# A two-layer convolution and window-attention kernel: layer 0's TensorE work regrouped by tile shape, with the normalisation moved ahead

## The chip, the core and the metric

The kernel runs on one core of a Trainium2 chip. The metric is the device time of one execution in microseconds; before the change its median over three runs is 3106.57 us (3105.86 to 3109.45). Engines are named as in the profile: PE is TensorE (PEld its weight loads), DVE is VectorE, ACT is ScalarE, POOL is GpSimd, SP is SyncE, which issues most DMAs. L403 is line 403 of the kernel before.

## The reference, cut to what matters

The input x is (2, 128, 256, 256) in float32: two images of 128 channels. Layer 0 adds halo attention to x, layer 1 adds the product of two small convolutions. Only layer 0 is touched by the change.

```python
WS, OWS, HEADS, DH = 8, 12, 4, 32       # 8x8 windows of queries, 12x12 of keys
def layer0(x, W_qkv, W_out, rel_height, rel_width):
    qkv = einsum('bchw,oc->bohw', x, W_qkv)
    q, k, v = split(qkv, 3, axis=1)
    q = windows(q) * DH ** -0.5; k = unfold_windows(k); v = unfold_windows(v)
    attn = q @ k.T + rel_pos_emb(q, rel_height, rel_width) + FIXED_MASK
    out = softmax(attn) @ v
    return einsum('bchw,oc->bohw', out, W_out)
x = x + layer0(group_norm(x), ...)
x = x + layer1(group_norm(x), ...)      # 5x1 convolution, depthwise 3x1, times a dilated 1x3
```

FIXED_MASK leaves each query only the keys whose row and column offsets have one parity. So the pixels fall into classes by the parities of row and column, and a query meets the 6x6 keys of its class.

## The kernel before, in words

**Strips and units.** Layer 0 (attention_fast) goes over 64 strips of 8 image rows, 32 for each image. A strip k has two units u = 2k and 2k + 1, one for each row parity r; 128 units in all. A unit holds both column parities c and 16 pairs of windows. Everything is float32, and each matmul of the code is two matmul and two weight-load instructions on TensorE.

**What a unit does.** The order on every engine is the order in the code (manual_schedule, L538), so the loop at L545 is the order of the work:

- In even units, load_rows fetches strip k + 2 (SP, 1280 KB), and normalise(k + 1) writes the normalised strip k + 1 by cells into one of two buffers xn: a GpSimd copy of the old rows (L308), four VectorE operations of 512 columns (L317), two copies of shared columns (L322, L323).
- In odd units of the first image, input_stats takes statistics of a strip of the second image (VectorE, four operations, L117), and load_next issues the next such load into the one buffer sx. Three strips' statistics stand elsewhere (units 4 and 8).
- by_place (GpSimd, four copies, L331) lays half of strip k + 1 out as xq for its coefficients; old_keys (GpSimd, L342) copies keys that two strips share.
- biases (L443): 16 matmuls in 32x64 tiles add the relative-position coefficients and the masks into the score banks.
- scores (L459): 64 matmuls in 64x64 tiles; ScalarE takes the exponentials in four pieces (L468).
- values (L424): 16 matmuls of 128 columns with the whole 128x128 array; ScalarE and VectorE copy one half of each bank to the tile vt (L430).
- coefficients (L403) of strip k + 1: 16 matmuls of 64 columns in 128x64 tiles into one bank; ScalarE (L412) and then VectorE (L416) copy one half each.
- attend (L484): 64 matmuls of 66 columns in 128x32 tiles, in three banks; VectorE divides by the sums (L490, L491), and turn transposes (L502).
- queries and keys of unit u + 1 and project of unit u (all L349): products with the whole array. in_parts cuts each bank's 512 columns into several matmuls: queries into three (one in the first unit of an image), keys and projection into two. result_stats takes the statistics of the unit before, and project adds the input (VectorE, L518) and stores the unit by SP.

All banks of values, coefficients, attention, queries, keys and projection come from one pool of four PSUM banks (tag pj), given out in turn: each needs the release of the bank given out four before it. At unit 8 VectorE computes six small sums of layer 1's weights (Weights.sums, L609 to L612). The two group norms that fall into this loop (of x of the second image, and of the first image's result) run in seven steps, one at each call of step().

**What follows.** convolutions_fast is layer 1; it starts when layer 0's last strips are stored.

## Time and profile before

| what | value |
|---|---|
| median of 3 runs | 3106.57 us |
| the profiled execution's own span | 3104.3 us (clock 0.996) |
| median of the runs above this span | 2.3 us |
| TensorE busy, matmuls and as many weight loads | 96%, 52,006 each |
| VectorE, ScalarE, GpSimd busy | 82%, 55%, 18% |
| first unit's biases; layer 1's first matmul | 107.9 us; 2103.4 us |
| a usual unit of layer 0 | 15.47 us |
| packets that bring TensorE's instructions (queue q8) | 412, 6.75 MB |

How to read it: the profile gives one execution. A view called the chain of work follows back from the last instruction what released each step, and shows the pieces with their start and length; "issue" in it is time in which the engine waited for nothing that the profile shows. The groups view gives busy time and mean length for each line of code, the waits view who waited for whom, and the timeline the instructions in order of time. Matmuls are pipelined, and their ends are modelled, so I compare starts with starts.

### The profile page before, as it was taken

What the parts mean: (1) busy time and instruction counts of PE and PEld (TensorE: products, weight loads), DVE (VectorE), ACT (ScalarE), POOL (GpSimd) and SP (SyncE); (2) the same over time, 40 slices, a digit from 0 to 9 for tenths busy, and PEclk for the clock granted to TensorE, in tenths of its full rate; (3) what the DMA queues carried; (4) which work ended last, traced back from release to release, by engine and by line L of the source; (5) the groups of instructions that cost most, each with busy time, mean ns of one, the idle gap of its engine ahead of it and who ended that gap; (6) DMA issues with size and microseconds to landing.
All of it is one profiled execution on the core that took longest, in us unless ns stands there. A gap on an engine that the chain in (4) does not pass through costs nothing.

```text
span 3104.3 us, 116029 instructions
## 1 busy us (share of the span) xinstructions
PE 2971.1 (96%) x52006; PEld 2248.5 (72%) x52006; DVE 2533.3 (82%) x4092; ACT 1711.4 (55%) x2673; POOL 569.0 (18%) x921
## 2 busy tenths in 40 slices
PE   0799999999999999999999999998999999999998
PEld 0688888888888888888888888884444444444443
DVE  8788888888888878777777777767999999999998
ACT  0455555555555555555555555555666665666664
POOL 2222222222222222222222222210000000000001
PEclk9999999999999999999999999999999999999999
DMA  9433333333333222222222222215788888888886
GB/s 395 160 125 128 111 115 111 115 112 115 111 115 112 84 71 87 72 86 72 88 71 87 71 88 71 84 37 168 206 217 213 221 216 213 222 215 214 217 217 167
DMA packets 137401, 434.75 MB, mean 140 GB/s; under 512 B 12993, under 2 KB 87617, under 8 KB 104385
## 3 DMA queue, kind: packets, MB, share of 16 engines
q1 hardware_dynamic: 127824, 361.18, 34.1%
q0 software_dynamic: 9072, 66.06, 11.5%
q8 instruction: 412, 6.75, 0.9%
q14 instruction: 93, 0.75, 0.1%
HBM read 284.59 MB, written 134.22 MB: 135 GB/s over the span
## 4 chain that ended last, share of the span: by engine, by line
PE 92%; DVE 2%; issue 1%; DMA 1%; ACT 0%; POOL 0%; SPq 0%; DVEq 0%; POOLq 0%; ACTq 0%
PE f_pv L424 15%; PE a_e L723 10%; PE a_o L723 10%; PE f_pq L349 9%; PE f_s L459 8%; PE f_o L484 8%; PE f_pk L349 7%; PE f_py L349 7%; PE f_pa L403 4%; PE f_s L443 4%; PE a_d L759 3%; PE b L799 2%; PE a_c L723 2%; PE g L704 2%; DVE t L788 0%
## 5 line engine op out<-in xcount | busy, mean ns | idle before, releaser
L430 DVE COPY f_vt<-f_pv 64x512 f32<-64x512 f32 x512 | 354.6, 695 | 290.7 <-ACT f_vt L430 290.5
L424 PE MATMUL f_pv<-f_wqkvT,f_xn 128*128 128x128 f32 x4096 | 491.3, 278 | 0.0
L468 ACT ACTIVATE f_p<-f_s 128x512 f32<-128x512 f32 x512 | 264.3, 603 | 404.1 <-PE f_s L459 404.1
L384 ACT ACTIVATE f_q<-f_pq,f_head 128x512 f32<-128x512 f32 x512 | 309.9, 687 | 303.0 <-PE f_pq L349 303.0
L424 PEld LDWEIGHTS f_pv<-f_wqkvT,f_xn 128*128 128x128 f32 x4096 | 466.9, 192 | 8.6
L331 POOL COPY f_xq<-f_xn 128x256 f32<-128x256 f32 x512 | 309.9, 649 | 757.9 <-DVE f_xn L317 757.9
L430 ACT COPY f_vt<-f_pv 64x512 f32<-64x512 f32 x512 | 297.4, 582 | 118.0 <-PE f_pv L424 117.8
L781 ACT ACTIVATE t<-t,w 128x1024 f32<-128x1024 f32 x128 | 147.0, 1149 | 375.2 <-DVE t L776 369.5
L788 DVE SCALAR_TENSOR_TENSOR t<-t,w,t 128x1024 f32<-128x1024 f32 x256 | 329.8, 1288 | 7.4 <-ACT t L781 1.3
L459 PEld LDWEIGHTS f_s<-f_q,f_kt 64*64 64x64 f32 x16384 | 250.6, 135 | 49.2 <-issue 49.2
L349 PE MATMUL f_pq<-f_xn,f_wq_s 128*128 128x192 f32 (+2 forms) x1520 | 277.0, 329 | 3.3 <-DVE f_xn L317 2.5
L459 PE MATMUL f_s<-f_q,f_kt 64*64 64x64 f32 x16384 | 268.1, 220 | 0.0
L484 PE MATMUL f_o<-f_vt,f_p 128*32 128x66 f32 x16384 | 264.2, 222 | 0.8 <-DVE mean_x L131 0.3
L484 PEld LDWEIGHTS f_o<-f_vt,f_p 128*32 128x32 f32 x16384 | 242.4, 110 | 10.4 <-DVE f_cf L416 1.0
L349 PE MATMUL f_pk<-f_xn,f_wqkvT 128*128 128x256 f32 x1024 | 245.2, 380 | 0.0
L349 PEld LDWEIGHTS f_pq<-f_xn,f_wq_s 128*128 128x128 f32 x1520 | 232.3, 188 | 16.9 <-issue 4.2
L349 PE MATMUL f_py<-f_ot,f_woT 128*128 128x256 f32 x1024 | 241.7, 378 | 2.3 <-DVE f_ot L502 2.3
L723 PE MATMUL a_e<-xm,w1s 128*128 128x512 f32 x512 | 240.7, 591 | 0.0
L723 PE MATMUL a_o<-xm,w1s 128*128 128x512 f32 x512 | 240.5, 590 | 0.2 <-ACT both L754 0.2
L308 POOL COPY f_xn<-f_xn 128x1280 f32<-128x1280 f32 x62 | 86.4, 1394 | 770.8 <-PE f_pv L424 770.8
L817 POOL DMA_DIRECT2D y<-f_x x63 | 54.5, 866 | 925.1 <-DVE y L809 910.1
L518 DVE TENSOR_TENSOR f_x<-f_py,f_raw 128x512 f32<-128x512 f32 x256 | 176.0, 688 | 57.9 <-PE f_py L349 50.2
(131 smaller groups left out, 4674.7 us busy)
## 6 DMA issues: line engine op xcount, KB each, us to landing
f_raw<-in_x SPq DMA_DIRECT2D x62, 1280.0 KB, 7.5
f_sx<-in_x SPq DMA_DIRECT2D x64, 1024.0 KB, 12.4
f_x<-f_x SPq DMA_DIRECT2D x128, 512.0 KB, 3.3
y<-f_x POOLq DMA_DIRECT2D x63, 1024.0 KB, 7.9
out<-y SPq DMA_DIRECT2D x63, 1024.0 KB, 4.0
raw<-f_x SPq DMA_DIRECT2D x64, 640.0 KB, 6.4
raw<-f_x SPq DMA_DIRECT2D x62, 384.0 KB, 7.7
t<-t4p SPq DMA_DIRECT2D x192, 32.0 KB, 4.3
```

The source lines that it names most:

```text
L331: nc.gpsimd.tensor_copy(xq[:, t2, half].rearrange("p t r n c e -> p r t (n c) e"), cells[:, :, 16 * half : 16 * half + 16, 1 + t2 : 9 : 4, ...
L349: nc.tensor.matmul(dst[:, 32 * lo : 32 * hi], w, moving[:, lo:hi], start=True, stop=True)
L384: nc.scalar.activation(q[:, c, :, i], pq.rearrange("p (n x) -> p n x", n=NPAIR), AF.Copy, scale=head[:, i : i + 1],)
L424: nc.tensor.matmul(pv[:, P * n : P * n + P], xn[k % 2][:, r, 4 * j + n].rearrange("p c x -> p (c x)"), wvT, start=True, stop=True,)
L430: (nc.vector.tensor_copy if c else nc.scalar.copy)(vt[rows, 4 * j : 4 * j + 4, :, c, 0:32], pv[rows].rearrange("p (n h d) -> p n h d", n=4 ...
L459: nc.tensor.matmul(sc[g][n // 8][64 * c : 64 * c + 64, n % 8].rearrange("p i x -> p (i x)"), keys_k[rows, c, 48 * n : 48 * n + 64], qs[u][ ...
L468: nc.scalar.activation(pts[u][:, g, 8 * half : 8 * half + 8].rearrange("p n i x -> p (n i x)"), sc[g][half].rearrange("p n i x -> p (n i x ...
L484: nc.tensor.matmul(po[32 * h : 32 * h + 32, n - lo], p[:, h // 2, n, h % 2], vt[:, n, h], start=True, stop=True,)
L518: nc.vector.tensor_tensor(x1[:, :, c:W:2], py.rearrange("p (m t) -> p t m", t=4), raws[k][:, r:8:2, c:W:2], ALU.add,)
L723: nc.tensor.matmul(pa[:, : n * W], w, rows, start=i == 0, stop=i == len(terms) - 1)
L781: nc.scalar.activation(t3[:, j : j + 4], t1[:, j : j + 4, :], AF.Copy, scale=w3[:, 0:1])
L788: nc.vector.scalar_tensor_tensor(t3[:, j : j + 4], t1[:, j + tap : j + tap + 4, :], w3[:, tap : tap + 1], t3[:, j : j + 4], ALU.mult, ALU.add,
```

## The change

The six kinds of TensorE work in a unit get a new order: biases (32x64 tiles), scores (64x64), coefficients and attention (both 128x32), then queries, keys, values and projection (all with the whole array). For this the values of unit u + 1 are made in unit u, behind its queries and keys, and those of unit 0 ahead of the loop. The coefficients take 32 matmuls of 64 columns with 32 weight columns each, in place of 16 with 64, and VectorE copies its half first. Strip k + 2, and not k + 1, is normalised, in odd units, in two halves: the first ahead of the coefficients, the second behind turn; its layout by GpSimd follows. Input statistics move to even units, also in halves, and the next input load is issued after the second. result_stats moves up behind the scores. Queries, keys and projection take one matmul of 512 columns a bank. The weights' sums go from VectorE to GpSimd. The calls of step() stand at other places.

```diff
@@ attention_fast: when statistics and norm steps are due
-                stats_at[2 * (b * NS + s) + 1] = b + 1, s
-            stats_at[2 * (b * NS + 2)] = b + 1, NS - 1
-            stats_at[2 * (b * NS + 4)] = b + 1, NS - 2
-            norm_at[2 * (b * NS + NS - 2) + 1] = st_x, b + 1, f"x{b + 1}"
+                stats_at[2 * (b * NS + s)] = b + 1, s
+            stats_at[2 * (b * NS + 2) + 1] = b + 1, NS - 1
+            stats_at[2 * (b * NS + 4) + 1] = b + 1, NS - 2
+            norm_at[2 * (b * NS + NS - 2)] = st_x, b + 1, f"x{b + 1}"
             norm_at[2 * ((b + 1) * NS + 2) + 1] = st_y, b, f"y{b}"
@@ input_stats
-            norm.chunk(st_x[b], 4 * s, sxs.pop(u))
+            t = sxs.pop(u)
+            def part(half):
+                norm.chunk(st_x[b], 4 * s + 2 * half, t[:, 4 * half : 4 * half + 4])
+                if half:
+                    load_next()
+            return [lambda half=half: part(half) for half in range(2)]
@@ normalise: the same operations, returned as two functions
+            def first():
+                old_rows()
+                pixels(0)
+            def second():
+                pixels(1)
+                shared()
+            return first, second
@@ keys, queries, project
-                in_parts(2, pk, wkT, inner(k, r, c, 2, 6))
+                in_parts(1, pk, wkT, inner(k, r, c, 2, 6))
-                in_parts(3 if u % (2 * NS) else 1, pq, wq_s, inner(k, r, c, 1, 5))
+                in_parts(1, pq, wq_s, inner(k, r, c, 1, 5))
-                in_parts(2, py, woT, ots.pop((u, c)).rearrange("p (n x) -> p n x", n=NPAIR))
+                in_parts(1, py, woT, ots.pop((u, c)).rearrange("p (n x) -> p n x", n=NPAIR))
@@ coefficients
                 for half in range(2):
-                    nc.tensor.matmul(
-                        pa[64 * half : 64 * half + 64, 64 * t : 64 * t + 64],
-                        wb[:, t2, t1].rearrange("p h x -> p (h x)"),
-                        xq[:, t2, half, t1].rearrange("p r n c e -> p (r n c e)"), start=True, stop=True,
-                    )
+                    for g in range(2):
+                        rows = slice(64 * half + 32 * g, 64 * half + 32 * g + 32)
+                        nc.tensor.matmul(
+                            pa[rows, 64 * t : 64 * t + 64],
+                            wb[:, t2, t1, 2 * g : 2 * g + 2].rearrange("p h x -> p (h x)"),
+                            xq[:, t2, half, t1].rearrange("p r n c e -> p (r n c e)"),
+                            start=True, stop=True,
+                        )
-            for i in range(2):
+            for i in (1, 0):
@@ the loop
-            normalise(0)
+            emit(normalise(0))
             by_place(0, range(4))
             emit(queries(0) + keys(0))
             coefficients(0, 0)
             coefficients(0, 1)
+            emit(lambda j=j: values(0, j) for j in range(4))
+            emit(normalise(1))
+            by_place(1, (0, 1))
             for u in range(NU):
...
-                if r == 0:
-                    if k + 2 < NB * NS:
-                        load_rows(k + 2)
-                    if more:
-                        normalise(k + 1)
+                if r == 0 and k + 2 < NB * NS:
+                    load_rows(k + 2)
+                aside = []
                 if u in stats_at:
-                    input_stats(u)
-                    load_next()
+                    aside.append(input_stats(u))
+                if r == 1 and k + 2 < NB * NS:
+                    aside.append(normalise(k + 2))
...
                 step()
-                if more:
-                    by_place(k + 1, (2 * r, 2 * r + 1))
                 if later:
                     old_keys(u + 1)
                 biases(u)
                 scores(u)
-                for j in range(4):
-                    values(u, j)
-                step()
+                if u > 0:
+                    result_stats(u - 1)
+                emit(first for first, _ in aside)
                 if more:
                     coefficients(k + 1, r)
                 step()
                 attend(u)
                 step()
                 turn(u)
                 step()
+                emit(second for _, second in aside)
+                if r == 0 and more:
+                    by_place(k + 1, (2, 3))
+                elif r == 1 and k + 2 < NB * NS:
+                    by_place(k + 2, (0, 1))
                 if later:
                     emit(queries(u + 1) + keys(u + 1))
+                    step()
+                    emit(lambda j=j: values(u + 1, j) for j in range(4))
                 step()
-                if u > 0:
-                    result_stats(u - 1)
                 project(u)
                 step()
@@ Weights.sums: six operations
-        self.nc.vector.tensor_add(self.w1s[:, 0], w[1], w[3])
+        self.nc.gpsimd.tensor_add(self.w1s[:, 0], w[1], w[3])
...
```

More of the change, by code (lines that the diff above doesn't have):

```diff
@@ L303, in normalise, with old_rows, pixels @@
             flat = cells.rearrange("p r a j i -> p (r a) j i")
-            if s == 0:
-                nc.gpsimd.memset(flat[:, :, :, 0:1], 0.0)
-                lo = 0
-            else:
-                nc.gpsimd.tensor_copy(
-                    flat[:, :, :, 0:2],
-                    by_cell(k + 1).rearrange("p r a j i -> p (r a) j i")[:, :, :, 4:6],
-                )
-                lo = 1
+            lo = 0 if s == 0 else 1
             hi = min(10, H - 8 * s) // 2
             rows = raws[k].rearrange("p (i r) (n j c) -> p r c n j i", r=2, n=NPAIR, c=2)
-            for r in range(2):
+            new = slice(1 + lo, 1 + hi)
+            def old_rows():
+                if s == 0:
+                    nc.gpsimd.memset(flat[:, :, :, 0:1], 0.0)
+                else:
+                    nc.gpsimd.tensor_copy(
+                        flat[:, :, :, 0:2],
+                        by_cell(k + 1).rearrange("p r a j i -> p (r a) j i")[:, :, :, 4:6],
+                    )
+                if hi < 5:
+                    nc.gpsimd.memset(flat[:, :, :, 1 + hi : 6], 0.0)
+            def pixels(r):
                 for c in range(2):
@@ L320, in normalise, with shared @@
                     )
-            new = slice(1 + lo, 1 + hi)
-            nc.vector.tensor_copy(cells[:, :, 2:32, 0, new], cells[:, :, 0:30, 8, new])
-            nc.vector.tensor_copy(cells[:, :, 0:30, 9, new], cells[:, :, 2:32, 1, new])
-            if hi < 5:
-                nc.gpsimd.memset(flat[:, :, :, 1 + hi : 6], 0.0)
+            def shared():
+                nc.vector.tensor_copy(cells[:, :, 2:32, 0, new], cells[:, :, 0:30, 8, new])
+                nc.vector.tensor_copy(cells[:, :, 0:30, 9, new], cells[:, :, 2:32, 1, new])
+            def first():
[5 more added lines that the diff above has]
+            return first, second
         def by_place(k, columns):
@@ L402, in coefficients @@
                 for half in range(2):
-                    nc.tensor.matmul(
-                        pa[64 * half : 64 * half + 64, 64 * t : 64 * t + 64],
-                        wb[:, t2, t1].rearrange("p h x -> p (h x)"),
-                        xq[:, t2, half, t1].rearrange("p r n c e -> p (r n c e)"), start=True, stop=True,
-                    )
+                    for g in range(2):
[5 more added lines that the diff above has]
+                            start=True, stop=True,
+                        )
             src = pa.rearrange("p (t m e) -> p e m t", t=8, e=2)
-            for i in range(2):
+            for i in (1, 0):
                 dst = cfs[k][..., i, 8 * r : 8 * r + 8].rearrange("p e r n c t -> p e (r n c) t")
@@ L543, in attention_fast @@
             coefficients(0, 1)
+            emit(lambda j=j: values(0, j) for j in range(4))
+            emit(normalise(1))
+            by_place(1, (0, 1))
             for u in range(NU):
                 k, r = divmod(u, 2)
-                b, s = divmod(k, NS)
                 later, more = u + 1 < NU, k + 1 < NB * NS
-                if r == 0:
-                    if k + 2 < NB * NS:
-                        load_rows(k + 2)
-                    if more:
-                        normalise(k + 1)
+                if r == 0 and k + 2 < NB * NS:
+                    load_rows(k + 2)
+                aside = []
                 if u in stats_at:
-                    input_stats(u)
-                    load_next()
+                    aside.append(input_stats(u))
+                if r == 1 and k + 2 < NB * NS:
+                    aside.append(normalise(k + 2))
                 step = lambda: None
@@ L608, in sums @@
         w = [self.w1[:, i] for i in range(5)]
-        self.nc.vector.tensor_add(self.w1s[:, 0], w[1], w[3])
-        self.nc.vector.tensor_scalar(self.w1s[:, 1], w[3], -1.0, None, ALU.mult)
+        self.nc.gpsimd.tensor_add(self.w1s[:, 0], w[1], w[3])
+        self.nc.gpsimd.tensor_scalar(self.w1s[:, 1], w[3], -1.0, None, ALU.mult)
         for i, (a, b) in enumerate(((2, 1), (4, 3), (0, 1), (2, 3))):
-            self.nc.vector.tensor_sub(self.w1s[:, 2 + i], w[a], w[b])
+            self.nc.gpsimd.tensor_sub(self.w1s[:, 2 + i], w[a], w[b])
 def convolutions_fast(tc, io, x1_d, norm, st_y, out, weights, count_good):
```

## The prediction

> **What bounds the kernel now.** I read the busy line and the instruction queue of the page first, then the chain of work over one unit (one strip and row parity) in the middle of layer 0, then the starts of the single matmuls in it, then the chain where a unit is not like the others. The busy line, the queue that loads instructions (packets, MB, share of the DMA engines):

> ```profile
> PE 2971.1 (96%) x52006; PEld 2248.5 (72%) x52006; DVE 2533.3 (82%) x4092; ACT 1711.4 (55%) x2673; POOL 569.0 (18%) x921
> q8 instruction: 412, 6.75, 0.9%
> ```

> The chain of work over one unit (start, us, what):

> ```profile
> 1012.80 1.05 PE f_s L443 x32
> 1013.85 2.02 PE f_s L459 x128
> 1015.87 3.77 PE f_pv L424 x32
> 1019.64 1.08 PE f_pa L403 x32
> 1020.72 1.98 PE f_o L484 x128
> 1022.70 2.08 PE f_pq L349 x12
> 1024.78 1.75 PE f_pk L349 x8
> 1026.54 1.73 PE f_py L349 x8
> ```

> No engine but TensorE is in it, and it has no gap: the pieces add to 15.46, and the biases of nearly every unit start 15.466 or 15.467 us after those before. So layer 0 (128 units, to about 2098 us) is bound by TensorE's order of instructions; the rest is layer 1, which the diff leaves alone. VectorE has room, TensorE none:

> ```profile
> 1012.73:1028.19 15.46, 13.09 (x23) 1.00 0.33 105
> 1028.19:1043.66 15.47, 12.20 (x24) 1.00 0.11 37
> ```

> (VectorE's busy time in an even and an odd unit, the granted clock 1.00, the DMA share). The third thing to see is a unit where the chain has a hole that no semaphore explains, "issue":

> ```profile
> 711.02 0.52 PE f_o L484 x25
> 711.54 0.12 issue
> 711.67 1.70 PE f_o L484 x103
> ```

> and the one instruction packet between 709.2 and 710.3, on a DMA system that a row load keeps full:

> ```profile
> q1 hardware_dynamic: 45, 0.45, 99.1%
> q8 instruction: 1, 0.02, 5.3%
> ```

> **Instruction blocks.** 52,006 matmuls, as many weight loads and some 1,100 waits in 412 packets are 255 instructions a packet; take 256. A unit has 380 matmuls, 380 weight loads and 8 waits: 768, three blocks exactly, so a new block begins at the same places in every unit: in the output projection, in the scores (2.35 us after the biases' start) and some 50 instructions into the attention product (8.30 us). The hole above stands there, and two others: the attention product took 2.06 and 2.11 instead of 1.98 us in the units at 641.1 and 1698.8. I set each packet beside the block it could bring. For 375 blocks the first matmul came 1.44 us or more after the packet's end; the three least, 1.44, 1.46 and 1.51 us, are the three stalls. And after each stall the next packet began 1.06 to 1.15 us after the stalled block was entered. So: **entering a block starts the load of the next one, and no further one.** From the entry in the scores of odd units the packet starts after 1.17 us (median) and takes 0.93; with 1.45 until use a block is ready **3.55 us** after the one before was entered. In even units, where the 1280 KB row load runs from 1.4 to 8.8 us, it starts after 2.42 us and takes 0.95: **4.82 us** (worst tenth: 3.16 and 1.52, 6.1 us). Now 256 dense instructions take 2.0 us (scores 2.02, attention product 1.98). The order of before never issues two blocks in a row that fast: 320 dense instructions (biases, scores), 3.77 us of values (64 instructions), 320 dense ones (coefficients, attention), 5.5 us with 56.

> [...]

> **The change, step by step** (all starts to starts of single matmuls).
> 1. *Six groups of one tile shape become four.* At each change the last interval of the old group and the first of the new are longer than the pitch: scores to values 149 for 39 and 213 for 112 ns (+211), values to coefficients +93+49, coefficients to attention +101+25, attention to queries +113+104, project to biases 145, biases to scores 184: 1.025 us. After: 217, 145 and 184 stay, and scores to coefficients, which this trace does not have, gets 110 (as the scores end now) + 25 (as attention begins; both ends by the other rows: 93+25 and 135+104): 0.681 (0.66 to 0.79). **-0.34 us** a unit (-0.24 to -0.36).
> 2. *Coefficients in 32 columns*: 16 pairs at 58.3 ns become 16 quads; the nearest row, attention's quads of 66 columns, has 57.6: -0.01 (0 if the pitch of the pairs stays, -0.03 by 64/66 of attention's).
> 3. *Parts*: queries' 160 and 192 columns go at 148 and 177 ns; unit 64 already has them whole, 468.5 ns: 1.889 becomes 1.874. Keys and projection: 220 and 215 ns for 256 columns, doubled at most: 0 to -0.01 each. **-0.03** in all. Steps 1 to 3: -0.38 x 126 = **-48 us**.
> 4. *VectorE's part of the coefficients first.* The first query bank waits for both evictions, as the rows at 1005.33 (ScalarE, 0.78) and 1006.14 (VectorE, 0.81) show: 0.30 after the last matmul, 1.59 of copies with 0.03 between, 0.15 to the matmul (a copy's end at 178.29, the matmul at 178.43) make 2.06 us, against 1.99 for attention and its exit. 0.07 a unit, 0 to 0.15; a stall elsewhere in the unit covers it: 0 taken (+8 if no block is late).
> 5. *Normalising two ahead, in halves; statistics; values' copies.* The same VectorE work: 13.1 and 12.2 per unit, now some 14.1 in an odd unit (4.3 of normalising, no input statistics) and 12.2 in an even one, of 15.08. Laid out in order, its coefficient eviction is due 4.26 us into the unit and VectorE is free at 3.8; the values' banks are given back over 1 us before the projection needs them. Cost 0. GpSimd's copies have over 5 us; the next input load (6.2 to 6.7 us to land) is issued 8 us ahead of its use. Were this cover gone, each 0.1 us costs 13.
> 6. *The weights' sums to GpSimd, strips' statistics at other units*: the unit at 233.5 took 20.95, that at 170.6 16.42 us; 6.4 us of stalls become about 0.65 in each of units 5 and 9: **-5**. GpSimd idles some 12 us a unit, so its six small operations (0.27 to 0.63 each on VectorE) hide even at twice that.
> 7. *Norm steps*: the second small matmul now waits behind all of attention's normalising, and the aggregate (3.61 us) delays the coefficients' eviction, whose bank the third attention bank needs: x about +3 (unit was +1.48 and +0.71), y about +5: **+8**, bounds 0 and +12.
> 8. *Start and end*: the prologue now has values, a second normalising (4.3) and four GpSimd copies (2.5) ahead of the first unit's coefficients; TensorE waits some 3.5, of which the shorter unit gives back part; at the end attention follows scores at once and waits 0.4 twice for the exponentials: **+2**. Within a unit they are done 3.5 us in, 0.5 before attention asks.
> 9. *Blocks.* A unit gets 396 matmuls: 800 instructions, so block starts wander through it, 32 instructions a unit; and biases, scores, coefficients and attention, 704 of them, now run together in 6.0 us. The first block start in the dense run was loaded during the slow half. The second comes 2.05 us later and waits 3.55-2.05 = 1.5 us (even units 2.7); the third, where the first lay in the run's first 192 instructions (three in four), waits about as long after the restart. Of the second ones some 15% count nothing, their block having been called for during the projection. 0.85+0.75 = 1.6 stalls a unit: 2.4 us odd, 4.3 us even, mean 3.35, x 126 = **+422 us**. Bounds: if the sequencer runs 64 instructions (0.5 us) ahead, as at the attention product, where the packet starts 0.64 and not 1.17 us after the entry, and the row load delays half as much, 2.4 a unit, +302; with the worst tenth's loads in even units, 4.45, +560. Nothing hides it: in the dense run TensorE has no other work.

> Sum: 3104.3 -48 -5 +8 +2 +422 = 3483 of span; the runs' median stands 2.3 above the span: **3486 us**.

> **Rivals.**
> - *Blocks are not late* (loads run ahead when instructions are short, or start earlier). For it: no stall in 372 of 375 blocks. Against: the three that came latest. Then 3104.3-48+8-5+8+2 = 3069 of span, 3072, faster. It decides where a block is ready within 2.0 us of the entry before it; with 2.2 to 2.3 us there is no gain left.
> - *Lighter stalls*, the lower bound: 3104.3-43+302 = 3363, 3366.
> - *Heavier*: the even units' loads at the upper bound, 3624; or stalls near 3 us bring the clock down as after the 3.9 us wait at 240 us, where coefficient pairs went from 58 to 106 ns: 3600 to 3750.
> - *VectorE becomes the bound* in odd units (14.1 of 15.08) or attention waits for its whole exponential tile (0.5 a unit): 3072+63 = 3135. Against: GpSimd's copies start on normalised rows before that tile's last copies have run, so waits go by regions.
> - *The shape changes cost the same in any order*: the forecast +43.

> **Chances.** Forecast (3400 to 3590) 0.62; lighter 0.15; heavier 0.12; blocks in time 0.09; the others 0.02. The range 3340 to 3640 leaves out the blocks in time and the heavier end. Faster by over 0.2% (about what a measurement of this kernel can tell from no change) 0.09, within 0.01, slower 0.90.

> **What would show it.** Right: "issue" in the chain of most units, 1.3 to 3 us long, at places that move by 32 instructions from unit to unit, even units longer than odd; units of some 18.5 us; the instruction packets one block behind; the shape changes at 0.68 a unit in what is left. Wrong: a period near 15.1 us with no "issue"; holes at the first query that VectorE or ScalarE ends; an odd unit longer than an even one.

## The result and the profile after

The changed kernel takes **3574.27 us** (median of 4 runs, 3570.88 to 3584.05) against 3107.94 us of the kernel before in the same session: a ratio of **1.1505**, 95% interval 1.1488 to 1.1522. It is 466 us slower where 379 were forecast, and inside the range. The profiled execution's span is 3569.1 us, 464.8 longer than that of before.

From the page of the changed kernel: the busy line, the queue that loads instructions (packets, MB, share), the chain by engine, and two lines of the costliest groups (busy us, mean ns, idle us ahead of them and what ended it):

```profile
PE 3053.5 (86%) x54070; PEld 1959.9 (55%) x54070; DVE 2552.8 (72%) x4086; ACT 1728.3 (48%) x2673; POOL 567.1 (16%) x927
...
q8 instruction: 428, 7.01, 0.8%
...
PE 84%; issue 11%; DVE 2%; ACT 0%; DMA 0%; POOL 0%; SPq 0%; DVEq 0%; ACTq 0%; POOLq 0%
...
L506 PE MATMUL f_o<-f_vt,f_p 128*32 128x66 f32 x16384 | 329.2, 236 | 292.1 <-issue 291.2
...
L424 PE MATMUL f_pa<-f_xq,f_wb 128*32 128x64 f32 x8192 | 157.8, 221 | 86.0 <-issue 83.4
```

The attention product's line in the page of before has next to no idle time:

```profile
L484 PE MATMUL f_o<-f_vt,f_p 128*32 128x66 f32 x16384 | 264.2, 222 | 0.8 <-DVE mean_x L131 0.3
```

TensorE fell from 96% to 86% of a longer span, and no engine took its place: VectorE is at 72%. The idle time is in two places, the coefficients (L424) and the attention product (L506), and nothing that the profile shows ended it.

The chain of work over one even unit in the middle of layer 0 (start, us, what; line numbers are those of the changed kernel):

```profile
1028.39 1.05 PE f_s L465 x32
1029.44 2.02 PE f_s L481 x128
1031.47 0.46 PE f_pa L424 x20
1031.93 0.72 issue
1032.65 0.81 PE f_pa L424 x42
1033.45 0.02 PE f_o L506 x2
1033.47 0.04 PE f_pa L424 x2
1033.51 1.17 PE f_o L506 x82
1034.68 3.74 issue
1038.42 0.89 PE f_o L506 x44
1039.31 3.26 PE f_pq L372 x4
1042.56 2.11 PE f_pk L372 x4
1044.68 3.57 PE f_pv L446 x32
1048.25 1.72 PE f_py L372 x4
```

A unit of before was eight pieces without a gap, 15.47 us. This one takes 21.58. It has two holes, 256 instructions apart; the second lasts 3.74 us, and behind it the queries take 3.26 us where the units before and after it have 2.07: TensorE's granted clock is 0.67 from 1038.42 to 1042.50. The pieces without a hole are shorter than before, as the change meant them to be (values 3.57 for 3.77, keys 1.73 for 1.75 in the other units).

I set all starts of layer 0 beside the instruction packets, as the prediction did for before:

```
                                            before           after
block starts with a hole over 0.35 us       0 of 382         197 of 398
us in holes, units 2 to 125                 0                410.3 (1.1 of it not at a block start)
holes a unit, odd and even                  -                1.56 and 1.54
us of holes a unit, odd and even            -                2.62 and 4.15
packet's end to the block's first matmul    1.44 or more     1.40 at a hole (middle 80%: 1.25 to 1.53)
```

(A start counts as a hole when its interval is over 0.35 us and is not the ordinary 0.43 to 0.47 us of a 512-column matmul, as it is at 12 further starts.) So the holes are late instruction blocks, nearly to the last microsecond: each ends 1.4 us (median) after the packet it waited for, and the next packet starts 1.05 us or more (median 1.18 in odd and 1.69 in even units) after the hole's end. From unit to unit their place moves back by 31 instructions and not by the 32 forecast: the records have 396 matmuls, 396 weight loads and 7 waits a unit, 799 in all, one wait fewer than was counted. Counted so, nearly every hole stands at the same remainder of 256, through all of layer 0: in units 2 to 125, 188 stand at one or other of two neighbouring remainders. Those units hold 124 x 799 = 99,076 instructions, 387.0 times 256, and 387 packets of q8 start in them, of 16,384 bytes each; before, with 124 x 768, it is 372 and 372. So the 256, which was taken from 255 instructions a packet, is what both traces show.

**Where the 465 us are.** The first unit begins 1.9 us later, layer 1 ends 1.1 later relative to layer 0, and the first two and last two units take 3.4 more; the rest is in units 2 to 125. Their pieces free of holes make 15.03 us in place of 15.467, -54; holes +410; what is left is +115, against 12.5 that before had in single units (the sums, the norms): +102. Of those 115 us, 87 lie in the 55 units whose longest hole is 2.5 us or more (1.16 us a unit where it is 2.5 to 3, 1.89 where it is over 3). Most of it is the clock: the windows around a hole at 1073.4 (us, TensorE's busy time, granted clock, DMA share, GB/s):

```profile
1067.59:1073.40 5.81, 5.12 (x278) 1.00 0.66 204
1073.40:1077.60 4.20, 0.10 (x6) 0.97 0.39 162
1077.60:1081.60 4.00, 3.94 (x78) 0.60 0.02 4
```

After the hole the clock is at 0.60 for 4 us, and attention's quads of four matmuls go at some 110 ns (median) in place of 57. The clock records of the trace give the whole amount. In units 2 to 125 they hold 50 stretches at half clock, 225 us in all (before: one, 3.4 us). Between 33 and 41 us of this lie in holes, by how a hole's start is taken; taking the work in the rest at twice its time, as the 110 ns for 57 suggest, I estimate a cost of 92 to 96 us (half of 225 less 33 to 41).

The length of a hole alone does not decide. In the clock records of these units every such stretch lasts 3.41 us (34 of them) or 6.83 us (16), and all begin on one grid of 3.41 us steps. Of the full-clock steps in these units, none of 571 with less than 2.0 us of idle TensorE was followed by a step at half clock, 3 of 13 with 2.0 to 2.2 us were, and 47 of 48 with 2.2 us or more. So it matters how a hole lies in the steps: of the block holes of 2.2 to 3.0 us that began at full clock, all 6 that lay in one step were followed by half clock, and 10 of the 35 that two steps shared. The mean granted clock of the whole span went from 0.996 to 0.965.

### The profile page after: what moved, and what is told of

Its sections match the earlier page's. It is cut to its first block, busy times and chain, and to the rows that moved or that the text cites. A ratio compares the mean times of both kernels' runs of the same rounds, so it can differ in the third digit from the quotient of the medians.

```text
span 3569.1 us, 119974 instructions
## 1 busy us (share of the span) xinstructions
PE 3053.5 (86%) x54070; PEld 1959.9 (55%) x54070; DVE 2552.8 (72%) x4086; ACT 1728.3 (48%) x2673; POOL 567.1 (16%) x927
## 4 chain that ended last, share of the span: by engine, by line
PE 84%; issue 11%; DVE 2%; ACT 0%; DMA 0%; POOL 0%; SPq 0%; DVEq 0%; ACTq 0%; POOLq 0%
PE f_pv L446 13%; PE a_e L749 9%; PE a_o L749 9%; PE f_pq L372 9%; PE f_o L506 8%; PE f_s L481 7%; PE f_pk L372 6%; PE f_py L372 6%; PE f_pa L424 4%; PE f_s L465 4%; PE a_d L785 3%; PE b L825 2%; PE a_c L749 2%; PE g L730 2%; DVE t L814 0%
## 5 line engine op out<-in xcount | busy, mean ns | idle before, releaser
L506 PE MATMUL f_o<-f_vt,f_p 128*32 128x66 f32 x16384 | 329.2, 236 | 292.1 <-issue 291.2
L446 PEld LDWEIGHTS f_pv<-f_wqkvT,f_xn 128*128 128x128 f32 x4096 | 476.5, 192 | 63.1 <-issue 60.1
L446 PE MATMUL f_pv<-f_wqkvT,f_xn 128*128 128x128 f32 x4096 | 477.8, 275 | 0.1
L506 PEld LDWEIGHTS f_o<-f_vt,f_p 128*32 128x32 f32 x16384 | 290.2, 119 | 313.6 <-issue 311.7
L372 PE MATMUL f_pq<-f_xn,f_wq_s 128*128 128x512 f32 x512 | 323.6, 760 | 5.4 <-issue 2.5
L512 DVE RECIPROCAL f_rc<-f_o 128x10 f32<-128x10 f32 (+1 forms) x384 | 84.2, 219 | 318.8 <-PE f_o L506 318.8
L438 DVE TENSOR_SCALAR f_cf<-f_pa,f_keep 128x512 f32<-128x512 f32 x128 | 103.8, 811 | 215.7 <-PE f_pa L424 215.6
L372 PE MATMUL f_pk<-f_xn,f_wqkvT 128*128 128x512 f32 x512 | 247.7, 604 | 0.0
L372 PE MATMUL f_py<-f_ot,f_woT 128*128 128x512 f32 x512 | 241.0, 593 | 1.7 <-DVE f_ot L524 1.7
L424 PE MATMUL f_pa<-f_xq,f_wb 128*32 128x64 f32 x8192 | 157.8, 221 | 86.0 <-issue 83.4
```

The lines of the kernel that those rows point to most:

```text
L372: nc.tensor.matmul(dst[:, 32 * lo : 32 * hi], w, moving[:, lo:hi], start=True, stop=True)
L424: nc.tensor.matmul(pa[rows, 64 * t : 64 * t + 64], wb[:, t2, t1, 2 * g : 2 * g + 2].rearrange("p h x -> p (h x)"), xq[:, t2, half, t1].rea ...
L446: nc.tensor.matmul(pv[:, P * n : P * n + P], xn[k % 2][:, r, 4 * j + n].rearrange("p c x -> p (c x)"), wvT, start=True, stop=True,)
L506: nc.tensor.matmul(po[32 * h : 32 * h + 32, n - lo], p[:, h // 2, n, h % 2], vt[:, n, h], start=True, stop=True,)
```

## The experiments

**Theory.** Entering a block of 256 instructions loads only the next one, and 256 instructions of dense small matmuls take 2.0 us, less than the 3.55 us (4.82 in even units) that the trace of before gave from a block's entry until the next is ready; putting the slow whole-array products in one place leaves 704 dense instructions in a row. **Rivals:** the new tile form or the other moves (VectorE's order, normalising two ahead) cost the time; or any number of instructions off a multiple of 256 does. Where one run was made, the kernel before ran beside it and took 3107.5 or 3108.9 us; runs of one kernel here differ by up to 0.6% (3104.0 to 3122.5 us in b_best).

### The values back between scores and coefficients

```diff
                 scores(u)
+                emit(lambda j=j: values(u, j) for j in range(4))
                 if u > 0:
                     result_stats(u - 1)
                 emit(first for first, _ in aside)
...
                     emit(queries(u + 1) + keys(u + 1))
                     step()
-                    emit(lambda j=j: values(u + 1, j) for j in range(4))
```

> The changed kernel with one thing undone: a unit's values stand between its scores and the coefficients again. Theory (late instruction blocks): 800 instructions a unit, so block starts still wander, but 3.6 us with only 64 instructions now part a dense run of 320 from one of 384. Without stalls a unit would take some 15.23 us; a block start in the first 128 instructions of the 384 still calls for the next block too late, and one in the first 64 of the 320. I work out 0.8 to 0.9 stalls a unit and 1.2 to 1.5 us of them, longer in even units than in odd ones, with about 0.2 us lost to a lower clock: 16.6 to 16.9 us a unit, 3250 to 3290 us in all, and each stall at a block start. Rival (the coefficients' new tile form, the normalising two ahead or VectorE's order makes the time, not the long run): all of these are still there, so it stays above 3450 us. Rival (any number of instructions that is no multiple of 256 costs the same, wherever the dense part lies): as many stalls a unit as in the changed kernel, 1.55, above 3450 us.

Measured: 3506.9 us, only 67 below the changed kernel. A miss, and it looks like the rivals' result. The waits of TensorE in it (us in total, times, longest) say what it is:

```profile
PE f_pq L372 <- DVE f_rc L512: 181.4, 100, 3.2
PE f_o L506 <- issue: 99.2, 94, 1.9
```

The block holes in the attention product fell from 291 to 99 us, but a new wait took most of the gain: the first query waits for VectorE. Its chain in an odd unit:

```profile
1013.75 3.78 PE f_pv L446 x32
...
1018.23 0.70 DVE f_vt L452
...
1018.96 1.29 DVE st_y L117 x2
1020.25 1.32 DVE f_xn L331 x2
...
1021.60 0.81 DVE f_cf L438
1022.41 0.15 DVE f_rc L512
```

VectorE copies the values, then does 2.6 us of statistics and normalising, and only then frees the coefficients' bank and attention's. In the changed kernel those operations lie behind the scores, where VectorE has nothing else to do. The clock is down in this run as well: the records hold 191 us at half clock in units 2 to 125, though no wait of the attention product for a block is over 1.9 us; the first query's waits are up to 3.2. My undoing of one part had broken another, so I undid it again with VectorE's work out of the way (first and second halves behind turn, the result's statistics ahead of the projection):

> The run with the values between scores and coefficients again, now with VectorE's other work out of their way: in that run VectorE had the values' copies, the result's statistics and a half of the normalising ahead of the coefficients' eviction, and the first query waited for it (181 us in all). Here both halves stand behind turn, and the result's statistics ahead of the projection, as before the change. Theory (late blocks): the waits for VectorE go, and what stays are stalls at block starts, 0.8 to 1.0 a unit, 1.2 to 1.6 us of them, and about 0.2 us of lower clock: 16.6 to 17.0 us a unit, 3250 to 3300 us. Rival (the coefficients' tile form or the normalising two ahead makes the time): above 3450 us as in the changed kernel.

Measured: 3380.9 us; that wait is down to 8 us. It is 81 above the upper end, and 193 below the changed kernel. Holes: 1.03 us a unit in odd units, as worked out, but some 2.7 to 2.8 in even ones, where the packets of the second dense part start 2.4 to 5.1 us after the call (medians; 0.9 to 1.9 in odd units): I put this down to the row load, as the run with fewer rows below suggests; I had taken 1.3 us of delay for it. The shortest unit is 15.54, not 15.23, because the first query now comes 2.30 us after the last coefficient, waiting for the two evictions. What is left is 0.3 a unit; the clock records have 150 us at half clock in these units. So undoing the grouping, with VectorE's work moved out of the way, takes back 193 of the 466 us, and a unit of 800 instructions with a shorter dense run is still slow.

### A unit of 768 instructions, and 60 instructions ahead of the loop

Coefficients in pairs and the old parts of queries, keys and projection bring the changed order back to 768 instructions a unit. The second kernel adds cuts to one product that runs once, ahead of the loop:

```diff
-                in_parts(3 if u % (2 * NS) else 1, pq, wq_s, inner(k, r, c, 1, 5))
+                in_parts(3 if u % (2 * NS) else 16 if u + c == 0 else 1, pq, wq_s, inner(k, r, c, 1, 5))
```

> The changed kernel with the coefficients in 128x64 pairs and the old parts of queries, keys and projection, so that a unit has 768 instructions again and blocks start at the same places in all units, while the values stay with the other whole-array products. Theory (late blocks): the dense run is 640 instructions, and blocks start some 184, 440 and 696 instructions into the unit (from where they start in the changed kernel's first unit, less 120 instructions of prologue). The second follows the first by 256 dense instructions, and the third lies in the slow half: one stall a unit, always at the same place in the attention product, some 0.6 to 1.0 us in odd units and 1.9 to 2.5 in even ones. With 15.19 us without stalls, 16.4 to 16.9 a unit, 3225 to 3290 us in all. Rival (shape changes, waits for other engines): places do not repeat and the time has nothing to do with a prologue; with the coefficients' old form about 3070 if that form was the cause, above 3450 if the order was.

> The kernel of the run before, with 15 more cuts in the first of unit 0's query products, ahead of the loop: 60 more instructions once, and not an instruction more in any unit. Theory (late blocks): blocks now start some 124, 380 and 636 instructions into each unit, all three of them in the dense run of 640, so two stalls a unit: some 2.0 to 2.4 us in odd units and 4.0 to 4.7 in even ones, with a lower clock behind the longer ones. 18.4 to 19.3 us a unit, 3480 to 3600 us in all, 200 to 330 more than without the 60 instructions. Rival (anything but the places of the blocks): the same time as the run before within 3 us.

Measured: 3304.9 and 3374.0 us. The first has one block hole in practically every unit (1.02 and 1.03 a unit), 1.87 us in even and 1.39 in odd units; 15 above the upper end, because the odd ones are not 0.6 to 1.0. Giving back the instruction counts alone thus takes back 269 us, more than undoing the grouping alone did. Undoing both, further below, takes back 444: the two work through the same block starts, and their shares do not add. Nearly all of it is at the attention product:

```profile
PE f_o L503 <- issue: 171.0, 124, 2.9
```

The second is 69 us slower for 60 instructions executed once. That is less than the 200 I expected at least, and the trace shows why: a unit has 767 instructions and not 768 (one wait fewer), so the places move on by one a unit. Only the first thirty to forty units have two late blocks, as worked out for all of them (18.6 us a unit in units 2 to 31); later the kernel passes through the places that the first one had earlier. This makes the better test. The same place in two kernels, 72 units apart:

```
block starts in the unit at     202            214            220            226
first kernel: unit, us          24: 17.29      36: 17.04      42: 16.87      48: 16.79
with the 60: unit, us           96: 17.31      108: 17.04     114: 16.85     120: 16.77
```

The unit's time follows the place of the block start to 0.02 us, in units 72 apart. In units 24 to 48 VectorE also takes input statistics, in 96 to 120 it does not, and the times agree all the same.

The same 60 instructions in the kernel before:

> The kernel before with the same 15 more cuts in the first of unit 0's query products, and nothing else: 60 more instructions ahead of the loop, 768 in each unit as before. Theory (late blocks): blocks now start some 185, 441 and 697 instructions into each unit, in place of 245, 501 and 757, so the second stands near the end of the coefficients and the third at the end of the attention product, and some of them come late: 0.5 us in odd units, 1.4 in even ones, with an uncertainty of half of that, since a place 20 instructions later would have no stall at all: 3165 to 3290 us, 3220 taken. Rival (blocks are not what holds the kernel): 3107 within 3 us.

Measured: 3198.3 us, +89 where about +110 was taken, from nothing but a prologue 60 instructions longer. Every unit's code is as before; 0.71 us of holes a unit in even and 0.39 in odd units now stand at instruction 697, near the end of the attention product:

```profile
PE f_o L484 <- issue: 48.6, 90, 3.4
```

So the kernel before owes these 89 us to where its blocks begin: at 245, 501 and 757 in each unit, in place of 185, 441 and 697.

### The row load

```diff
-            t = rawp.tile([P, 10, W], F32, tag="raw", name=f"f_raw_{k}")
-            n = min(10, H - 8 * s)
+            if k < 3:
+                kept[k] = rawp.tile([P, 10, W], F32, tag="raw", name=f"f_raw_{k}")
+            t = kept[k % 3]
+            n = min(10, H - 8 * s) if k < 3 else 1
```

> The changed kernel with the row loads cut to one of their ten rows from the fourth strip on (128 KB in place of 1280; the other rows are those of the first three strips, so it computes on old data). Theory (late blocks, and the row load delays the packets in even units): the even units' stalls of 4.15 us fall to what odd units have, 2.6, and hardly any stall reaches the 3 us after which the clock halves; 15.05 + 2.65 + 0.3 = 18.0 us a unit in both parities, 3390 to 3470 us in all. Rival (the even units' longer stalls come from something else in them, such as the statistics on VectorE or the GpSimd layout): 3550 to 3575 us.

Measured: 3458.7 us, 116 below the changed kernel. Its waits, beside the 291.2 and 83.4 us of the changed kernel for the same two groups:

```profile
PE f_o L510 <- issue: 212.8, 123, 2.5
...
PE f_pa L428 <- issue: 81.2, 61, 2.8
```

The even units' holes fell from 4.15 to 2.84 us a unit, the odd ones' stayed (2.62 and 2.69). For blocks called for 3.1 to 6.9 us into an even unit the packet starts after 1.2 us in place of 2.1 (first image) and 2.4 (second). No hole of units 2 to 125 is longer than 3 us any more, and the time beside the holes fell from 115 to 73 us. It did not go to the 0.3 a unit I gave it: 78 units still have a hole of 2 to 3 us, and lose 0.75 each beside it. The 3 us after which the clock halves, in my expectation, was my estimate; no run shows it. The clock records speak against it: with no hole that long, 29 stretches at half clock, 109 us, are left.

### One part alone: the coefficients' tile form

```diff
                 for half in range(2):
-                    nc.tensor.matmul(
-                        pa[64 * half : 64 * half + 64, 64 * t : 64 * t + 64],
-                        wb[:, t2, t1].rearrange("p h x -> p (h x)"),
+                    for g in range(2):
+                        rows = slice(64 * half + 32 * g, 64 * half + 32 * g + 32)
+                        nc.tensor.matmul(
+                            pa[rows, 64 * t : 64 * t + 64],
+                            wb[:, t2, t1, 2 * g : 2 * g + 2].rearrange("p h x -> p (h x)"),
```

> The kernel before with one part of the change alone: the coefficients in 128x32 tiles, 64 matmul instructions in place of 32. Theory (late blocks): the matmuls themselves get 0.17 us a unit shorter (15.30 without stalls), but a unit has 832 instructions, so block starts move by 64 a unit, and the dense run of coefficients and attention has 384: 0.9 to 1.0 stalls a unit, 1.2 to 1.6 us of them, 16.6 to 17.0 us a unit, 3245 to 3300 us in all. Rival (the new tile form is a gain or a loss by itself, blocks don't matter): 3085 us if it is a gain of 0.17 a unit, and no stalls at block starts.

Measured: 3276.2 us. The coefficients take 0.918 us in place of 1.082, a gain of 0.164 a unit, and still the kernel is 169 us slower: 1.1 block holes a unit, 1.74 us in even and 1.00 in odd units. The form is good; the 64 instructions it adds are not.

### All the rest, without grouping and with the old instruction counts

> All of the change but its grouping and its instruction counts: the coefficients in pairs, the old parts, the values between scores and coefficients, but the normalising two ahead, VectorE's half of the coefficients first, the statistics at other units and the sums on GpSimd. Theory (late blocks): outside of the block stalls a unit takes 15.47 us as before, and units 5 and 9 have no stall from the sums. If a unit keeps 768 instructions with its waits, blocks stay where they were, and it takes 3095 to 3105 us; if a wait is gone (767, as in the two kernels with the pairs), blocks drift by one instruction a unit, and the later units get stalls of about 1 us at block starts: up to 3180. Rival (VectorE's order or the normalising two ahead costs 0.1 us or more a unit): a usual unit without a block stall takes 15.57 us or more.

Measured: 3130.1 us, +22.6. There are no block holes to speak of (2.6 us in all; blocks stayed at 245 and 235), and a usual unit takes 15.593: the rival's 15.57 or more. The chain of a unit shows the wait:

```profile
1500.92 3.78 PE f_pv L443 x32
...
1505.40 0.69 DVE f_vt L449
1506.10 0.03 issue
1506.13 0.82 DVE f_cf L435
1506.95 0.02 issue
1506.97 0.79 ACT f_cf L431
1507.76 0.04 issue
1507.81 2.15 PE f_pq L372 x12
```

VectorE's half of the coefficients comes first and stands behind VectorE's copy of the values, so it starts 0.58 us after the last coefficient; in the kernel before ScalarE's half came first, after 0.27 to 0.30. The first query is late by the difference less some slack: 0.126 us a unit, 16 us in all. In the changed kernel the copies of the values are elsewhere and VectorE starts after 0.26 to 0.31. So VectorE's order fits the grouped order and does harm in the other; the rest of the 22.6 is in the norm units and the start.

### What of it is worth keeping

> The kernel before with the weights' six sums on GpSimd in place of VectorE, and nothing else. Unit 8 took 5.48 us more than the others, waiting for them; GpSimd has room. Theory (my step 6): 5 to 5.5 us less, 3101.5 to 3103 us, a ratio of 0.998. Rival (the sums on GpSimd take so long that its next copies are late): a smaller gain, or 3107.

Measured: 3103.9 us (11 runs) against 3107.6 (23 runs), ratio 0.9989 (0.9981 to 0.9998): 3.7 less, short of the 5 to 5.5 expected. Unit 8 went from 20.95 to 16.43 us, so 4.5 of the 5.5 went; the 0.95 left is that of unit 4, which has no sums: the strip statistics that stand there.

> The run before it, with keys in one matmul a bank (2 before) and the projection in three (2 before): 768 instructions a unit as before, so blocks start where they did. Keys in one matmul took 1.730 us a unit in the changed kernel against 1.756, the projection 1.812 in one against 1.817 in two. Theory: 0.026 less a unit for the keys and 0.005 more for the projection, 0.02 x 126 = 2.6 us below the run before it: 3099 to 3100.5 us, a ratio of 0.997 to before. Rival (the cuts bring nothing, or blocks move into a stall): no less than the run before it, or 60 us and more if a stall comes.

Measured: 3112.4 us, ratio 1.0015 (1.0005 to 1.0025), slower than before. A usual unit did get shorter, 15.453, but even units of the first image have holes, in one line of the waits:

```profile
PE f_o L484 <- issue: 8.6, 10, 1.4
```

They stand at instruction 509, a block start; without the two cuts in unit 0's keys the prologue is 8 instructions shorter.

> The kernel with the sums on GpSimd and the new cuts of keys and projection, which came out slower: cutting unit 0's keys less had taken 8 instructions from the prologue, so blocks start at 253 and 509 in a unit, and not at 245 and 501, and ten even units of the first image got a stall of 0.7 to 1.6 us at 509. Here unit 0's queries are cut in two, which puts the 8 instructions back. Theory (late blocks): the stalls go, a usual unit stays at 15.453 us, and it is 0.014 x 126 = 1.8 us below the kernel with the sums alone: 3101 to 3103 us, a ratio of 0.998 to before. Rival (the new cuts themselves make those stalls): 3110 to 3113 us again.

Measured: 3101.5 us, ratio **0.9982** (0.9973 to 0.9991): the holes at 509 are gone, and this version is faster than both kernels, by 6 us than before. The 8 instructions made 11 us. With them missing, the packet called for in the scores of those units starts 3.27 us after the call (median), with them 2.33, before 2.35. That it slips behind a stretch of the row load is my reading; it was not tried by itself.

## Why the prediction was right, step by step

The forecast's mechanism and its main term held; its sum is 88 us short (3486 for 3574), and that lies in a term which it had left to a rival.

1. *Six groups to four, 2. coefficients, 3. parts*: -0.38 a unit forecast, -0.437 measured (15.03 for 15.467), -54 us in place of -48. Scores to coefficients is 148 ns between starts for a pitch of 39: 109 against the 110 taken; coefficients to attention 33 at most; the quads go at 55.8 ns and not 57.6.
4. *VectorE's half first*: right where it was put. ScalarE's copy ends 1.91 to 1.94 us after the last coefficient, with 0.15 to a matmul 2.06 to 2.09 (2.06 forecast), and the first query came no earlier than 3.39 us after it in any unit: a hole always covered it. In the order without grouping it costs 0.126.
5. *Normalising two ahead, in halves*: 0, right. That it hangs on VectorE's free time behind the scores was shown by the run without this cover: 181 us.
6. *Sums*: -5 forecast; alone they are worth -3.7 (0.6 to 5.9 by the interval).
7. *Norm steps*: +8 forecast. The units with them lose 3.2, 2.0 and 3.4 us beside their holes, 8.6 in all, against 3.8 in before: +4.8, within the bounds (some of it is again the clock).
8. *Start and end*: +2; +1.9 and +1.1, and 3.4 in the first two and last two units, their holes included.
9. *Blocks*: +422 forecast (1.6 holes a unit; 2.4 odd, 4.3 even, mean 3.35). Measured 1.55 holes, 2.62 and 4.15, mean 3.31 over 124 units: 410. The median hole is 1.75 us in odd and 2.58 in even units (1.5 and 2.7 forecast). The delay by the row load (packets 2.1 and 2.4 us after a call, 1.2 with fewer rows) and the fetch of one block ahead (387 block starts and 387 packets; behind a hole the next packet came 1.05 us or more after its end) showed as forecast. That the sequencer runs 64 instructions ahead, in the lower bound, was an estimate from 0.64 us in place of 1.17; for block starts in the changed kernel's attention product the next packet starts after 1.17 us (median). The move from unit to unit is 31 instructions, not 32, because a unit has 7 waits and not 8.

The term that was mis-sized is the one that the sum gives nothing: **the lower clock behind long holes**. The prediction named it ("stalls near 3 us bring the clock down") and put it among the heavier cases, at 3600 to 3750. By the estimate from the clock records it takes 92 to 96 us, which is the size of the whole miss; the blocks' 12 us less and the smaller differences above nearly cancel. I had worked with the mean length of a hole, 2.7 us in even units, and with a limit near 3, an estimate from one wait of 3.9 us in the trace of before. Neither fits: 32 units have a hole of over 3 us, 47 of 48 steps with 2.2 us of idle time or more were followed by half clock, and where the row loads were cut, holes that were all under 3 us left 29 stretches of it. The range held the time, but its upper part had been worked out for longer loads in even units and not for the clock; that much was luck.

*The rivals.* Blocks in time: refuted, by the 410 us of holes, which end 1.4 us (median) behind a packet. VectorE as the bound: not in the changed kernel, but it is what the order without grouping ran into. Attention waiting for its exponentials: 0.2 us in all. Shape changes at the same cost in any order: refuted by 15.03. Of the signs set down in advance, "issue" in most units, the steady move from unit to unit (31 instructions for 32), even units longer than odd (20.55 and 17.98 us, mean 19.3 for 18.5 forecast), and the packets a block behind were all found; the holes are up to 6.2 us long, not 3.

## What to carry to other kernels

In this kernel, whose TensorE is full of small matmuls, the array was not the only resource: instructions were the second. 256 dense ones took 2.0 us, and by the trace of before a block needed 3.55 us from its call to its use, 4.82 under a row load of 1280 KB. The slow, wide products between the dense parts paid for that (0 holes in 382 block starts), and regrouping by tile shape took them away (197 holes in 398). So in such a kernel count the instructions between block starts, and read both times from its own trace. With 768 instructions a unit, three times 256, the places of the block starts were part of the tuning: 60 instructions ahead of the loop moved them and cost 89 us, and 8 fewer cost a variant 11, so compare such edits at equal counts, or they are read as something they are not. And the holes cost more than their length: by my estimate from the clock records, 92 to 96 us at half clock on top of 410.
